# Context attention with its scores transposed: one context position per partition

## The chip, the cores and the metric

The kernel runs on one core of a Trainium2 chip. The metric is the device time of one execution in microseconds (us); the median of several runs is compared. TensorE (PE) multiplies matrices and loads its weights (PEld) beside the products; VectorE (DVE), ScalarE (ACT) and GpSimd (POOL) work elementwise; SyncE (SP) issues the loads.

## The reference, cut to what matters

All data is float32. There are 16 batches of 128 rows with 512 columns, and a context of 2048 positions per batch.

```python
def _L0_xattn_ref(hidden_states, visual_hidden_state):
    scores = jnp.einsum('bld,bvd->blv', hidden_states, visual_hidden_state)
    probs = jax.nn.softmax(scores, axis=-1)
    return jnp.einsum('blv,bvd->bld', probs, visual_hidden_state)
...
x = x + _L0_xattn_ref(_layernorm(x, axis=-1), ctx_1024)
x = x + _L0_attn_ref(_layernorm(x, axis=-1), L0_attn_Wq_down, ...)
x = x + _L0_ffn_ref(_layernorm(x, axis=-1), L0_ffn_Wr, L0_ffn_A, L0_ffn_Bw)
```

The second step is causal self-attention with 16 heads of 32 columns and rotary positions; the third sends each batch through the two of eight low-rank experts that its first row chooses.

## The kernel before

The work of a batch is cut into Python generators, and the kernel's last part calls their steps in an order written out by hand. `score(b)` makes the layer norm of x, its transpose hT, the context scores (psc), their maximum and the exponentials sc. `attend(b)` multiplies the exponentials with the context (av), divides by their sum and adds x. `inner(b)` is the self-attention: q, k and v, the head scores pss, their softmax att, the transposed probabilities (tr_p_a, copied to pT_a), the head outputs y and the output product o. `experts(b)` routes the batch (`shares`, `route`, with the small product lg) and applies the two experts (mid, ffn). `early(b)` routes the last batch ahead of its end.

The 2048 context positions come in four tiles of 512, once turned (ctxT, four at a time in SBUF) for the scores and once as they are (ctx, four at a time) for av. In `score`, a tile takes four products with 512 columns each: the weights are the four column blocks of hT, and the result has one query row per partition and 512 positions along it. VectorE (L220) moves a result from PSUM to sc and takes its maximum along the row in the same instruction. After the fourth tile one ScalarE instruction (L229) makes all 2048 exponentials of a row and their sum.

The product av needs the positions on the partitions. So `attend` transposes the exponentials 128 columns at a time on TensorE (tr_p, through `turn` and `transposed`, L93), and ScalarE copies each group of four out of PSUM (L126). Two groups are turned ahead of the first av.

The order on TensorE and on SP's queue at the start is kept as written. The instructions of the other engines are put in order by a scheduler, which also sets the waits. In the loop of 14 passes, pass b runs `inner(b)`, `attend(b+1)`, `score(b+2)` and `experts(b-1)` in turns. PSUM has eight banks of 512 columns: three in `ps_tr` (transposes and small products), two in `ps_sc` (psc, and the first two of the four head-score banks, pss_sc) and three in `ps_acc` (av, q, k, v, pss_acc, y, o, mid, ffn). A bank is given out again when all readers of its last content are done.

Names of tiles in the profile have no numbers: psc stands for every context score bank, tr_p for every transposed group of exponentials.

Of the kernel before, what the change touches and what calls it, by code (L numbers as in the profile page):

```python
# [11 lines left out]
F32 = mybir.dt.float32  # L12
I32 = mybir.dt.int32
U32 = mybir.dt.uint32
AF = mybir.ActivationFunctionType
ALU = mybir.AluOpType
AX = mybir.AxisListType
PSUM = bass.MemoryType.PSUM

P = 128  # L20
B, S, V, D = 16, 128, 2048, 512
# [3 lines left out]
KC = D // P  # L25
VC = V // 512
# [40 lines left out]
def perceiver_block(ctx: ExitStack, tc: tile.TileContext, io: dict, out: bass.AP):  # L67
    nc = tc.nc

    const = ctx.enter_context(tc.tile_pool(name="const", bufs=1))  # L70
    p1 = ctx.enter_context(tc.tile_pool(name="p1", bufs=1))
    p2 = ctx.enter_context(tc.tile_pool(name="p2", bufs=2))
    p3 = ctx.enter_context(tc.tile_pool(name="p3", bufs=3))
    p4 = ctx.enter_context(tc.tile_pool(name="p4", bufs=4))
    p5 = ctx.enter_context(tc.tile_pool(name="p5", bufs=5))
    ps_tr = ctx.enter_context(tc.tile_pool(name="ps_tr", bufs=3, space=PSUM))
    ps_sc = ctx.enter_context(tc.tile_pool(name="ps_sc", bufs=2, space=PSUM))
    ps_acc = ctx.enter_context(tc.tile_pool(name="ps_acc", bufs=3, space=PSUM))
# [3 lines left out]
    ident = cst[:, C_ID : C_ID + P]  # L82
    ones = const.tile([P, P], F32, name="ones")
# [5 lines left out]
    def matmul(*args, **kwargs):  # L89
        tc.keep_in_program_order(nc.tensor.matmul(*args, **kwargs))  # L90

    def transpose(*args):
        tc.keep_in_program_order(nc.tensor.transpose(*args))  # L93
# [9 lines left out]
    def bank(pool, tag, name):  # L103
        return pool.tile([P, 512], F32, tag=tag, name=name)
# [4 lines left out]
    def layernorm(src, name, n=P, tag="h"):  # L109
        stats = p2.tile([P, 6], F32, tag="stats", name=f"st_{name}")[:n]  # L110
        nc.vector.bn_stats(stats, src)
        mv = p2.tile([P, 2], F32, tag="mv", name=f"mv_{name}")[:n]
        nc.vector.bn_aggr(mv, stats)  # L113
        rstd = p2.tile([P, 1], F32, tag="rstd", name=f"rs_{name}")[:n]
        nc.gpsimd.tensor_scalar_add(rstd, mv[:, 1:2], EPS)  # L115
        nc.gpsimd.tensor_tensor(rstd, rstd, mhalf[:n], ALU.pow)  # L116
        h = (p2 if tag == "h" else p1).tile([P, D], F32, tag=tag, name=f"{tag}_{name}")[:n]
        nc.vector.tensor_scalar(h, src, mv[:, 0:1], rstd, ALU.subtract, ALU.mult)  # L118
        return h

    def transposed(src, dst, name, at=(0, 1, 2, 3)):

        tr = bank(ps_tr, "tr", f"tr_{name}")
        for c, i in enumerate(at):
            transpose(tr[:, c * P : (c + 1) * P], src[:, i * P : (i + 1) * P], ident)
        nc.scalar.copy(dst, tr.rearrange("p (c t) -> p c t", c=4))  # L126

    def turn(src, at, name):
        t = p5.tile([P, 4, P], F32, tag="pT", name=f"pT_{name}")
        transposed(src, t, f"p_{name}", at)  # L130
        return t

# [3 lines left out]
    def load_weight(n, tag="ctxT"):  # L136

        down[n] = []
        for g in range(2):
            t = p4.tile([P, 4, D], F32, tag=tag, name=f"down_{n}_{g}")  # L140
            load(
                t, io[f"W{n}_downT"][g * 512 : (g + 1) * 512].rearrange("(a p) c -> p a c", p=P)
            )
            down[n].append(t)
# [8 lines left out]
    def fold_products(i, n, g):  # L153
        banks = [bank(ps_acc, "acc", f"fold_{n}_{g}_{j}") for j in range(2)]
        for a in range(4):
            for j, ps in enumerate(banks):
                rows = slice(j * L, (j + 1) * L)
                matmul(
                    ps[a * DH : (a + 1) * DH, :], up[rows, i, :], down[n][g][rows, a, :],
                    start=True, stop=True,  # L160
                )
        folded = []
        for j, ps in enumerate(banks):
            t = p5.tile([P, D], F32, tag="pT", name=f"folded_{n}_{g}_{j}")
            (nc.vector.tensor_copy if j else nc.scalar.copy)(t, ps)
            folded.append(t)
        return folded
# [14 lines left out]
    scores, firsts, values, lasts, routes = {}, {}, {}, {}, {}  # L182


    def load_x(b):
        xs[b] = p3.tile([P, D], F32, tag="x", name=f"x_{b}")
        load(xs[b], io["x"][b])
# [3 lines left out]
    def load_turned(b, vs=range(VC)):  # L191
        for v in vs:
            t = p4.tile([P, KC, 512], F32, tag="ctxT", name=f"ctxT_{b}_{v}")
            load(t, io["ctxT"][b, v])
            turned_cts.setdefault(b, []).append(t)
# [11 lines left out]
    def score(b):  # L207

        h = layernorm(xs[b], f"1_{b}")
        yield  # L210
        hT = p2.tile([P, KC, S], F32, tag="hT1", name=f"hT1_{b}")
        transposed(h, hT, f"1_{b}")
        yield
        sc = p2.tile([P, V], F32, tag="sc", name=f"sc_{b}")
        mx = p2.tile([P, VC], F32, tag="mx", name=f"mx_{b}")
        for v, ct in enumerate(turned_cts.pop(b)):
            ps = bank(ps_sc, "sc", f"psc_{b}_{v}")
            for c in range(KC):
                matmul(ps, hT[:, c, :], ct[:, c, :], start=(c == 0), stop=(c == KC - 1))
            nc.vector.tensor_scalar(  # L220
                sc[:, v * 512 : (v + 1) * 512], ps, 1.0, None, ALU.mult, ALU.max,
                accum_out=mx[:, v : v + 1],
            )
            if v < VC - 1:
                yield
        nm = p2.tile([P, 1], F32, tag="nm", name=f"nm_{b}")
        nc.vector.tensor_reduce(nm, mx, AX.X, ALU.max, negate=True)  # L227
        den = p2.tile([P, 1], F32, tag="den", name=f"den_{b}")
        nc.scalar.activation(sc, sc, AF.Exp, bias=nm, accum_out=den)  # L229
        rden = p2.tile([P, 1], F32, tag="rden", name=f"rden_{b}")  # L230
        nc.vector.reciprocal(rden, den)
        scores[b] = (sc, rden)
        yield

    def attend(b):

        sc, rden = scores.pop(b)
        acc = bank(ps_acc, "acc", f"av_{b}")
        turned = [turn(sc, range(4 * i, 4 * i + 4), f"{b}_{i}") for i in range(2)]
        yield  # L240
        for v, ct in enumerate(cts.pop(b)):
            now = turned.pop(0)
            for j in range(4):
                matmul(
                    acc, now[:, j, :], ct[:, j, :],
                    start=(v == 0 and j == 0), stop=(v == VC - 1 and j == 3),
                )
            if v + 2 < VC:
                turned.append(turn(sc, range(4 * (v + 2), 4 * (v + 2) + 4), f"{b}_{v + 2}"))
            if v < VC - 1:  # L250
                yield
        x1 = p2.tile([P, D], F32, tag="x1", name=f"x1_{b}")
        nc.vector.scalar_tensor_tensor(x1, acc, rden, xs.pop(b), ALU.mult, ALU.add)  # L253
        firsts[b] = (x1, layernorm(x1, f"2_{b}"))
        yield

    def inner(b):
# [89 lines left out]
        def heads(c):  # L347
            first = c // 2 * 8 + c % 2 * 2
            return first, first + 1, first + 4, first + 5

        now = [turn(flat, heads(c), f"a_{b}_{c}") for c in range(HC)]
        yield
        acc = bank(ps_acc, "acc", f"y_{b}")
# [139 lines left out]
    def step(kind, b, n=1):  # L493
        if not 0 <= b < B:
            return
        if (kind, b) not in gens:
            gens[kind, b] = kind(b)
        for _ in range(n):
            next(gens[kind, b])
# [10 lines left out]
    step(score, 0, 5)  # L510
    step(score, 1, 2)
    step(score, 0)
    step(score, 1, 3)
    load_weight("q")
    load_weight("k")
    step(attend, 0, 2)
    step(score, 1)
    load_weight("v", "ctx")
    step(attend, 0, 3)
    load_x(2)  # L520
    step(score, 2)
    load_ctx(1, [0, 1])
# [18 lines left out]
    for b in range(B - 2):  # L541
        if 2 < b + 2 < B:
            load_turned(b + 2)
        step(inner, b, 2)
        step(experts, b - 1)
        step(score, b + 2)
        step(inner, b)
        step(experts, b - 1)
        step(score, b + 2, 3)
        step(attend, b + 1)  # L550
        step(inner, b)
        step(attend, b + 1, 2)
        step(score, b + 2)
        step(attend, b + 1)
        step(inner, b)
        step(attend, b + 1)
        if b + 2 < B:
            load_ctx(b + 2)
        if b + 3 < B:
            load_x(b + 3)  # L560
        step(inner, b)
        step(experts, b - 1)
        step(inner, b)
        step(inner, b + 1)
        step(experts, b - 1)
        step(score, b + 3)


    y, z = B - 2, B - 1
    step(inner, y, 2)  # L570
    step(experts, y - 1)
    step(inner, y)
    step(experts, y - 1)
    step(attend, z, 5)
    step(inner, y)
    step(experts, y - 1)
    step(inner, z)
    step(experts, y - 1)
    step(inner, z, 3)
    step(inner, y)  # L580
    step(early, z)
    step(inner, y)
    step(inner, z)
# [53 lines left out]
```

## Time and profile before

| | us |
|---|---|
| median of 3 runs | 886.39 |
| lowest and highest | 885.8, 887.42 |
| the profiled execution | 886.97 |
| its span, first to last instruction | 885.0 |
| mean granted TensorE clock | 0.994 of full speed |

Costly groups by line, of the profiled execution:

| line, engine | what | count | busy us | mean ns |
|---|---|---|---|---|
| L90 PE | av<-ctx,pT, 128x512 | 512 | 231.6 | 596 |
| L90 PE | psc<-ctxT,hT, 128x512 | 512 | 228.6 | 600 |
| L90 PE | q<-hT,w_q, 128x128 | 512 | 62.6 | 282 |
| L93 PE | tr_p<-cst,sc, 128x128 | 256 | 35.8 | 273 |
| L220 DVE | sc<-psc, 128x512 | 64 | 44.3 | 692 |
| L126 ACT | pT<-tr_p, 128x512 | 64 | 34.2 | 580 |
| L229 ACT | sc<-sc, 128x2048 | 16 | 32.1 | 2004 |

A product counts as two records on TensorE and on its weight loads, a transpose as one. Products are pipelined: a record is longer than the distance to the next one, so the cost of a stretch of TensorE is read from the starts. Times of engines other than TensorE overlap with it.

### The profile page before, as it was taken

Reading aid. Unit: us, or ns where it says so; the run is one execution under the profiler, and the core shown is the slowest. Engines: PE = TensorE matmul, PEld = TensorE weight load, DVE = VectorE, ACT = ScalarE, POOL = GpSimd, SP = SyncE. Lnnn points to the kernel's source line nnn. Section 1 sums busy time; section 2 is a strip of 40 time slices with the busy share of each in tenths; the row PEclk is TensorE's granted clock in tenths of the full one; section 3 lists DMA queues with packets and bytes.
Section 4 is the critical chain, followed back from the end, with each engine's and each line's share of the span. In section 5 each row is a group of like instructions: output and inputs, shape, how many; then the busy total and the mean of one; then the engine's idle time right before and its main releaser. Section 6 shows DMA issues by size and latency. Waiting matters only on the chain.

```text
span 885.0 us, 11267 instructions
## 1 busy us (share of the span) xinstructions
PE 857.5 (97%) x4138; PEld 503.1 (57%) x4138; DVE 429.1 (48%) x1122; ACT 265.1 (30%) x797; POOL 168.7 (19%) x232
## 2 busy tenths in 40 slices
PE   5999999999999999999999999999999999999896
PEld 2446564565657556565755656575565657556653
DVE  1135455354645535464453546446354644633563
ACT  0132413315142331514233151422315142241351
POOL 1001021130403103040210404021040402204124
PEclk9999999999999999999999999999999999999998
DMA  6997735646273564627356362745636273151002
GB/s 274 414 367 302 258 122 207 215 145 225 79 278 137 199 217 143 230 80 269 146 191 226 137 235 78 265 155 183 233 134 235 78 263 148 34 181 37 12 1 72
DMA packets 29542, 159.39 MB, mean 180 GB/s; under 512 B 4144, under 2 KB 4400, under 8 KB 13104
## 3 DMA queue, kind: packets, MB, share of 16 engines
q1 hardware_dynamic: 25392, 146.09, 44.6%
q0 software_dynamic: 4096, 12.59, 4.5%
q8 instruction: 33, 0.54, 0.2%
q14 instruction: 21, 0.17, 0.1%
HBM read 154.47 MB, written 4.19 MB: 179 GB/s over the span
## 4 chain that ended last, share of the span: by engine, by line
PE 94%; DVE 2%; ACT 1%; DMA 1%; POOL 1%; issue 1%; POOLq 0%; SPq 0%; ACTq 0%
PE psc L90 25%; PE av L90 25%; PE q L90 7%; PE k L90 6%; PE v L90 6%; PE o L90 5%; PE tr_p_a L93 3%; PE tr_p L93 3%; PE tr L93 2%; PE pss_sc L90 2%; PE y L90 2%; PE mid L90 2%; PE pss_acc L90 1%; PE ffn L90 1%; ACT att L335 1%; DMA x<-in_x_dram 1%
## 5 line engine op out<-in xcount | busy, mean ns | idle before, releaser
L90 PE MATMUL av<-ctx,pT 128*128 128x512 f32 x512 | 231.6, 596 | 0.5 <-ACT pT L126 0.5
L90 PE MATMUL psc<-ctxT,hT 128*128 128x512 f32 x512 | 228.6, 600 | 0.7 <-ACT hT L126 0.7
L90 PEld LDWEIGHTS psc<-ctxT,hT 128*128 128x128 f32 x512 | 95.9, 192 | 110.8 <-issue 109.8
L90 PEld LDWEIGHTS av<-ctx,pT 128*128 128x128 f32 x512 | 93.5, 190 | 105.6 <-issue 104.6
L220 DVE TENSOR_SCALAR_CACHE_REDUCE sc<-psc 128x512 f32<-128x512 f32 x64 | 44.3, 692 | 162.0 <-PE psc L90 162.0
L335 ACT ACTIVATE att<-att,nmx 128x128 f32<-128x128 f32 x256 | 99.0, 388 | 46.1 <-DVE nmx L333 46.1
L115 POOL TENSOR_SCALAR rs<-mv 128x1 f32<-128x1 f32 x48 | 10.7, 234 | 487.9 <-DVE mv L113 487.4
L126 ACT COPY hT<-tr 128x512 f32<-128x512 f32 x48 | 26.8, 587 | 196.2 <-PE tr L93 196.2
L126 ACT COPY pT<-tr_p 128x512 f32<-128x512 f32 x64 | 34.2, 580 | 157.2 <-PE tr_p L93 157.1
L90 PEld LDWEIGHTS q<-hT,w_q 128*128 128x128 f32 x512 | 60.0, 196 | 13.5 <-ACT hT L126 13.5
L90 PE MATMUL q<-hT,w_q 128*128 128x128 f32 x512 | 62.6, 282 | 4.0 <-ACT hT L126 4.0
L90 PE MATMUL o<-w_c,yT 128*128 128x512 f32 x128 | 59.5, 609 | 1.1 <-ACT yT L362 1.1
L90 PE MATMUL k<-hT,w_k 128*128 128x128 f32 x512 | 59.8, 275 | 0.0
L253 DVE SCALAR_TENSOR_TENSOR x<-av,rden,x 128x512 f32<-128x512 f32 x16 | 12.0, 751 | 97.9 <-PE av L90 97.9
L90 PEld LDWEIGHTS k<-hT,w_k 128*128 128x128 f32 x512 | 58.5, 192 | 0.0
L90 PE MATMUL v<-w_v,hT 128*128 128x512 f32 x128 | 57.6, 592 | 0.0
L118 DVE TENSOR_SCALAR h<-x,mv,rs 128x512 f32<-128x512 f32 x48 | 39.3, 819 | 37.3 <-POOL rs L116 36.3
L229 ACT ACTIVATE sc<-sc,nm 128x2048 f32<-128x2048 f32 x16 | 32.1, 2004 | 53.2 <-DVE nm L227 53.2
L335 ACT ACTIVATION_READ_ACCUMULATOR att<-att,nmx 128x1 f32 x256 | 47.9, 187 | 0.0
L93 PEld LDWEIGHTS tr_p<-cst,sc 128*128 128x128 f32 x256 | 31.0, 141 | 24.7 <-issue 24.7
L340 DVE TENSOR_TENSOR att<-att,rsm 128x512 f32<-128x512 f32 x64 | 44.1, 689 | 1.0
L407 POOL DMA_INDIRECT each<-in_A_dram,g_blocks x32 | 32.7, 1023 | 58.9 <-DVE g_dn L424 50.4
(114 smaller groups left out, 913.3 us busy)
## 6 DMA issues: line engine op xcount, KB each, us to landing
ctxT<-in_ctxT_dram SPq DMA_DIRECT2D x64, 1024.0 KB, 5.2
ctx<-in_ctx_dram SPq DMA_DIRECT2D x64, 1024.0 KB, 4.8
x<-in_x_dram SPq DMA_DIRECT2D x16, 256.0 KB, 5.8
out_dram<-out POOLq DMA_DIRECT2D x15, 256.0 KB, 2.4
down_q<-in_Wq_downT_dram SPq DMA_DIRECT2D x2, 1024.0 KB, 10.6
down_k<-in_Wk_downT_dram SPq DMA_DIRECT2D x2, 1024.0 KB, 8.3
down_v<-in_Wv_downT_dram SPq DMA_DIRECT2D x2, 1024.0 KB, 7.9
w_c<-in_Wc_dram SPq DMA_DIRECT2D x1, 1024.0 KB, 14.0
```

The costliest lines, as they stand in the source:

```text
L90: tc.keep_in_program_order(nc.tensor.matmul(*args, **kwargs))
L93: tc.keep_in_program_order(nc.tensor.transpose(*args))
L115: nc.gpsimd.tensor_scalar_add(rstd, mv[:, 1:2], EPS)
L118: nc.vector.tensor_scalar(h, src, mv[:, 0:1], rstd, ALU.subtract, ALU.mult)
L126: nc.scalar.copy(dst, tr.rearrange("p (c t) -> p c t", c=4))
L220: nc.vector.tensor_scalar(sc[:, v * 512 : (v + 1) * 512], ps, 1.0, None, ALU.mult, ALU.max, accum_out=mx[:, v : v + 1],)
L229: nc.scalar.activation(sc, sc, AF.Exp, bias=nm, accum_out=den)
L253: nc.vector.scalar_tensor_tensor(x1, acc, rden, xs.pop(b), ALU.mult, ALU.add)
L335: nc.scalar.activation(att[:, i, :], att[:, i, :], AF.Exp, bias=nmx[:, i : i + 1], scale=SCALE, accum_out=sm[:, i : i + 1],)
L340: nc.vector.tensor_tensor(att[:, hs, :], att[:, hs, :], rsm[:, hs, None].to_broadcast([P, 4, S]), ALU.mult)
L407: nc.gpsimd.indirect_dma_start(each[:, i, :], None, io["A"], bass.IndirectOffsetOnAxis(ap=blocks[:, i : i + 1], axis=0),)
```

## The change

The context scores are computed with the roles of the two operands exchanged. The weights are now 128x128 blocks of ctxT, the moving side is a block of hT with 128 columns, and a result has one context position per partition and the 128 query rows along it. A tile takes 16 products in place of 4. These scores lie as av needs them, so `attend` has no transposes and no copies of transposes.

The maximum and the sum of a query row now run across partitions. ScalarE copies each score bank to sc (L224), and VectorE takes the elementwise maximum over the tiles from PSUM (L227), then halves 512 to 128 columns in two steps (L232, L233). A transpose on TensorE (tr_m), a reduction along the row (L242), a diagonal matrix of the negative maxima (L244) and a product with ones (spread) bring each query's maximum to all partitions. VectorE adds it to the four parts of sc (L249), and ScalarE makes the exponentials of each part (L252). VectorE adds up the parts (L255 to L258); in `attend`, a product of this partial sum with ones (den) gives the sum of each row, whose reciprocal (L276) is used as before.

`score` has two steps more and `attend` one less, and the written order is changed to fit. In the loop the context scores of a batch are now split two and two around the head scores and the first av, where they were three and one; `attend` starts after the head scores. At the end, `attend` of the last batch takes turns with the head scores of the batch before. The tag pT has four buffers in place of five. What is loaded stays the same.

```diff
-            ps = bank(ps_sc, "sc", f"psc_{b}_{v}")
-            for c in range(KC):
-                matmul(ps, hT[:, c, :], ct[:, c, :], start=(c == 0), stop=(c == KC - 1))
-            nc.vector.tensor_scalar(
-                sc[:, v * 512 : (v + 1) * 512], ps, 1.0, None, ALU.mult, ALU.max,
-                accum_out=mx[:, v : v + 1],
-            )
+            ps = bank(ps_sc, "sc", f"psc_{b}_{v}").rearrange("p (j t) -> p j t", j=4)
+            for j in range(4):
+                for c in range(KC):
+                    matmul(
+                        ps[:, j, :], ct[:, c, j * P : (j + 1) * P], hT[:, c, :],
+                        start=(c == 0), stop=(c == KC - 1),
+                    )
+            nc.scalar.copy(sc[:, v], ps)
+
+            if v:
+                nc.vector.tensor_tensor(mx, ps, mx if v > 1 else sc[:, 0], ALU.max)
             if v < VC - 1:
                 yield
+
+        def halved(t, op):
+            nc.vector.tensor_tensor(t[:, :2], t[:, :2], t[:, 2:], op)
+            nc.vector.tensor_tensor(t[:, 0], t[:, 0], t[:, 1], op)
+            return t[:, 0]
+
+        most = halved(mx, ALU.max)
+        yield
+
+        tr = bank(ps_tr, "tr", f"tr_m_{b}")
+        transpose(tr[:, :S], most, ident)
         nm = p2.tile([P, 1], F32, tag="nm", name=f"nm_{b}")
-        nc.vector.tensor_reduce(nm, mx, AX.X, ALU.max, negate=True)
-        den = p2.tile([P, 1], F32, tag="den", name=f"den_{b}")
-        nc.scalar.activation(sc, sc, AF.Exp, bias=nm, accum_out=den)
-        rden = p2.tile([P, 1], F32, tag="rden", name=f"rden_{b}")
-        nc.vector.reciprocal(rden, den)
-        scores[b] = (sc, rden)
+        nc.vector.tensor_reduce(nm, tr[:, :S], AX.X, ALU.max, negate=True)
+        diag = p1.tile([P, S], F32, tag="diag", name=f"diag_{b}")
+        nc.vector.tensor_scalar(diag, ident, nm, None, ALU.mult)
+        yield
+        spread = bank(ps_tr, "tr", f"spread_{b}")
+        matmul(spread[:, :S], ones, diag, start=True, stop=True)
+        for v in range(VC):
+            nc.vector.tensor_tensor(
+                sc[:, v], sc[:, v], spread[:, None, :S].to_broadcast([P, 4, S]), ALU.add
+            )
+            nc.scalar.activation(sc[:, v], sc[:, v], AF.Exp)
+        sums = p1.tile([P, 4, S], F32, tag="sums", name=f"sums_{b}")
+        for v in range(1, VC):
+            nc.vector.tensor_tensor(sums, sc[:, v], sums if v > 1 else sc[:, 0], ALU.add)
+        part = p2.tile([P, S], F32, tag="part", name=f"part_{b}")
+        nc.vector.tensor_tensor(sums[:, :2], sums[:, :2], sums[:, 2:], ALU.add)
+        nc.vector.tensor_tensor(part, sums[:, 0], sums[:, 1], ALU.add)
+        scores[b] = (sc, part)
         yield
...
-        turned = [turn(sc, range(4 * i, 4 * i + 4), f"{b}_{i}") for i in range(2)]
-        yield
         for v, ct in enumerate(cts.pop(b)):
-            now = turned.pop(0)
             for j in range(4):
                 matmul(
-                    acc, now[:, j, :], ct[:, j, :],
+                    acc, sc[:, v, j, :], ct[:, j, :],
                     start=(v == 0 and j == 0), stop=(v == VC - 1 and j == 3),
                 )
-            if v + 2 < VC:
-                turned.append(turn(sc, range(4 * (v + 2), 4 * (v + 2) + 4), f"{b}_{v + 2}"))
+            if v == VC - 2:
+                den = bank(ps_tr, "tr", f"den_{b}")
+                matmul(den[:, :1], part, ones[:, :1], start=True, stop=True)
+                rden = p2.tile([P, 1], F32, tag="rden", name=f"rden_{b}")
+                nc.vector.reciprocal(rden, den[:, :1])
...
         step(score, b + 2)
         step(inner, b)
         step(experts, b - 1)
-        step(score, b + 2, 3)
+        step(score, b + 1)
+        step(score, b + 2, 2)
+        step(inner, b)
         step(attend, b + 1)
-        step(inner, b)
-        step(attend, b + 1, 2)
+        step(score, b + 2)
+        step(attend, b + 1)
         step(score, b + 2)
         step(attend, b + 1)
         step(inner, b)
+        step(score, b + 2)
         step(attend, b + 1)
...
     y, z = B - 2, B - 1
-    step(inner, y, 2)
+    step(inner, y)
+    step(score, z)
+    step(inner, y)
     step(experts, y - 1)
     step(inner, y)
     step(experts, y - 1)
-    step(attend, z, 5)
+    step(attend, z)
     step(inner, y)
+    step(attend, z, 3)
     step(experts, y - 1)
+    step(inner, y)
     step(inner, z)
     step(experts, y - 1)
     step(inner, z, 3)
-    step(inner, y)
```

In the start, which the diff leaves out here, the steps of `score` for batches 0 and 1 take turns in the same manner.

More of the change, by code (lines that the diff above doesn't have):

```diff
@@ L74, in perceiver_block @@
     p4 = ctx.enter_context(tc.tile_pool(name="p4", bufs=4))
-    p5 = ctx.enter_context(tc.tile_pool(name="p5", bufs=5))
     ps_tr = ctx.enter_context(tc.tile_pool(name="ps_tr", bufs=3, space=PSUM))
@@ L128, in turn @@
     def turn(src, at, name):
-        t = p5.tile([P, 4, P], F32, tag="pT", name=f"pT_{name}")
+        t = p4.tile([P, 4, P], F32, tag="pT", name=f"pT_{name}")
         transposed(src, t, f"p_{name}", at)
@@ L163, in fold_products @@
         for j, ps in enumerate(banks):
-            t = p5.tile([P, D], F32, tag="pT", name=f"folded_{n}_{g}_{j}")
+            t = p4.tile([P, D], F32, tag="pT", name=f"folded_{n}_{g}_{j}")
             (nc.vector.tensor_copy if j else nc.scalar.copy)(t, ps)
@@ L213, in score @@
         yield
-        sc = p2.tile([P, V], F32, tag="sc", name=f"sc_{b}")
-        mx = p2.tile([P, VC], F32, tag="mx", name=f"mx_{b}")
+        sc = p2.tile([P, VC, 4, S], F32, tag="sc", name=f"sc_{b}")
+        mx = p1.tile([P, 4, S], F32, tag="mx", name=f"mx_{b}")
         for v, ct in enumerate(turned_cts.pop(b)):
-            ps = bank(ps_sc, "sc", f"psc_{b}_{v}")
-            for c in range(KC):
-                matmul(ps, hT[:, c, :], ct[:, c, :], start=(c == 0), stop=(c == KC - 1))
-            nc.vector.tensor_scalar(
-                sc[:, v * 512 : (v + 1) * 512], ps, 1.0, None, ALU.mult, ALU.max,
-                accum_out=mx[:, v : v + 1],
-            )
+            ps = bank(ps_sc, "sc", f"psc_{b}_{v}").rearrange("p (j t) -> p j t", j=4)
[8 more added lines that the diff above has]
+                nc.vector.tensor_tensor(mx, ps, mx if v > 1 else sc[:, 0], ALU.max)
@@ L233, in score @@
+        nc.vector.tensor_tensor(part, sums[:, 0], sums[:, 1], ALU.add)
+        scores[b] = (sc, part)
         yield
     def attend(b):
-        sc, rden = scores.pop(b)
+        sc, part = scores.pop(b)
         acc = bank(ps_acc, "acc", f"av_{b}")
-        turned = [turn(sc, range(4 * i, 4 * i + 4), f"{b}_{i}") for i in range(2)]
-        yield
         for v, ct in enumerate(cts.pop(b)):
-            now = turned.pop(0)
             for j in range(4):
                 matmul(
-                    acc, now[:, j, :], ct[:, j, :],
+                    acc, sc[:, v, j, :], ct[:, j, :],
@@ L512, in perceiver_block @@
     step(score, 0)
-    step(score, 1, 3)
+    step(score, 1)
+    step(score, 0)
+    step(score, 1)
+    step(score, 0)
+    step(score, 1)
     load_weight("q")
     load_weight("k")
-    step(attend, 0, 2)
+    step(attend, 0)
+    step(score, 1)
+    step(attend, 0)
     step(score, 1)
     load_weight("v", "ctx")
-    step(attend, 0, 3)
+    step(attend, 0, 2)
     load_x(2)
```

## The prediction

> **What bounds the kernel now.** I read the busy times first, then the waits, then the timeline of TensorE over one batch of the steady loop, since a share over the whole span does not say which stage pays.
>
> ```profile
> PE 857.5 (97%) x4138; PEld 503.1 (57%) x4138; DVE 429.1 (48%) x1122; ACT 265.1 (30%) x797; POOL 168.7 (19%) x232
> ```
>
> TensorE is the bound; VectorE and ScalarE have half their time to spare. In the waits, TensorE itself waits 26 us in all, none of it repeated once per batch, and the only per-batch wait of its weight loads that touches the changed code is this one:
>
> ```profile
> PEld pss_sc L90 <- DVE sc L220: 2.4, 14, 0.2
> ```
>
> It says that in 14 batches the head scores pss, which share the two PSUM banks of ps_sc with the context scores psc, had to wait 0.2 us for the eviction of a psc. The timeline of TensorE (start, length, operation, count) from the routing product lg to the head outputs y of one batch:
>
> ```profile
> 237.56 0.28 PE L90 MATMUL lg<-g_part,ones 128*128 128x8 f32 x2
> 237.70 10.55 PE L90 MATMUL psc<-ctxT,hT 128*128 128x512 f32 x24
> 248.08 1.04 PE L93 MATMUL tr_p<-cst,sc 128*128 128x128 f32 x8
> 249.05 1.13 PE L90 MATMUL pss_sc<-kb,qT 64*128 64x256 f32 x8
> 250.01 1.03 PE L90 MATMUL pss_acc<-kb,qT 64*128 64x256 f32 x8
> 250.97 3.70 PE L90 MATMUL av<-ctx,pT 128*128 128x512 f32 x8
> 254.51 0.60 PE L93 MATMUL tr_p<-cst,sc 128*128 128x128 f32 x4
> 258.38 0.60 PE L93 MATMUL tr_p<-cst,sc 128*128 128x128 f32 x4
> 258.82 3.60 PE L90 MATMUL psc<-ctxT,hT 128*128 128x512 f32 x8
> 262.26 3.60 PE L90 MATMUL av<-ctx,pT 128*128 128x512 f32 x8
> 271.04 1.08 PE L90 MATMUL y<-pT_a,vv 128*32 128x128 f32 x32
> 277.78 3.82 PE L90 MATMUL q<-hT,w_q 128*128 128x128 f32 x32
> 281.43 3.74 PE L90 MATMUL k<-hT,w_k 128*128 128x128 f32 x32
> 285.01 1.04 PE L93 MATMUL tr<-cst,h 128*128 128x128 f32 x8
> ```
>
> No idle time stands in it, so a price on TensorE is the step from one start to the next. One 512-wide context tile costs 262.26 - 258.82 = 3.44 us (8 records are 4 products). The transposes tr_p cost 0.97 + 0.44 + 0.44 = 1.85 us. And q and k are exactly the form that the new scores take, 16 products with a 128x128 weight and 128 columns: 3.65 and 3.58 us. lg to y is 33.48 us. The period of the loop is 289.32 - 237.56 = 51.76 us.
>
> **Products (loop).** Per batch: 16 transposes go, -1.85. Four tiles go from 3.44 to 3.57 (k's rate), +0.52; at q's rate +0.84. Added: the transpose of the maxima (0.11, a sixteenth of tr_p_a's 1.82), the spread product (a sixteenth of k, 0.22), the sum product den (like lg, 0.14): +0.47. Products alone: -0.86 us per batch.
>
> **The wait that is added.** Before, after the last psc of the group came 0.97 us of tr_p, which covered the eviction: a psc ends issuing at 248.08, VectorE starts at 248.28, is done at 248.97, and pss_sc runs at 249.05.
>
> ```profile
> 248.28 0.69 DVE L220 TENSOR_SCALAR_CACHE_REDUCE sc<-psc 128x512 f32<-128x512 f32 x1 [2.73 <-PE psc L90]
> 237.76 0.59 ACT L292 COPY vv<-v 128x512 f32<-128x512 f32 x1 [2.80 <-PE v L90]
> ```
>
> After, TensorE's order is lg, spread, psc 0, psc 1, pss, av 0, psc 2, av 1, psc 3, av 2, den, tr_p_a, maxima, av 3. The transposes no longer stand between psc and pss; the first pss (0.24 us) takes the bank of psc 0, free since long, the second that of psc 1, which ended 0.24 us before. Psc 1 now has two readers, the copy on ScalarE (L224) and the maximum on VectorE (L227); in the built program the maximum waits for the copy of the same bank, and the second pss for the maximum. So, from psc 1's last issue: 0.20 to ScalarE's start (237.56 to 237.76 above), 0.59 copy, 0.03 (ScalarE's last exponential ends at 257.64, VectorE goes on at 257.67), 0.69 maximum (the 128x512 add out of PSUM, L326, has 685 ns), 0.08 back to TensorE: 1.59. Minus the 0.24 of the first pss, plus about 0.05 for a weight load that is not hidden: 1.40 us of idle TensorE per batch. Queued behind it are pss, all four av and the rest of the batch.
>
> The Trainium skill, PSUM — Partial Sum Buffer, section "PSUM bank collisions raise a hardware error", says that two engines must not read one bank at once. No trace here has two readers of a bank; by that rule the wait is unavoidable for this code, and without it, with the two reads side by side, the sum would have 0.78 in place of 1.40.
>
> **Is VectorE there in time?** From the spread on it holds four adds (0.60 apart, as the two L326 adds that take 1.29), about 2.4 of routing operations between them, three sums (two of them dependent, 0.73), a 256-wide half (0.42), a 128-wide one. I bound that last by a kb quarter (0.42) and a four-column operation (0.16), and take 0.25. Starting at 238.19 these end near 244.7; psc 1 ends at 245.1 and its copy at 245.9: VectorE has 1.2 us of slack, ScalarE more (four exponentials of 512 columns, bounded by 0.39 for 128 and 2.00 for 2048 of them, on the line between these 0.71 each). Were nothing overlapped, the maximum would be 0.3 late: upper bound of the wait 1.7; lower bound 0.78 if ScalarE's copy did not count (0.20 + 0.69 + 0.08 - 0.24 + 0.05). Kb is made before the spread, so pss has it.
>
> **Covered otherwise.** The chain psc 3, copy, maximum, two halves takes 2.3 us and has av 2, den and tr_p_a (5.4) in front of the transpose that needs it. Its reduction and the diagonal (bounds 0.16 and 0.82) have until the next batch's spread. The division needs den before x1: av 3 lies between. Loads: the same tiles on SP's queue; the third and fourth ctxT tile are released later by some us, with 50 us to the next use. Cost nothing.
>
> So per batch: -0.86 + 1.40 = +0.54. The bounds give -0.08 (wait 0.78) and +1.16 (wait 1.7 and q's rate). Fourteen loop batches: +7.6 us, from -1 to +16.
>
> **Start.** Eight tiles +1.0, tr_p -1.85 and its 0.24 us wait for the copy, small products +0.6: -0.4, with every maximum hidden behind the next tile.
>
> **End.** Before, pss of batch 14 stands after av of batch 15, and q of batch 15 waits for its layer norm and behind ScalarE's exponentials:
>
> ```profile
> 826.76 0.63 PE L93 MATMUL tr<-cst,h 128*128 128x128 f32 x4 [0.89 <-DVE h L118]
> 831.62 5.46 PE L90 MATMUL q<-hT,w_q 128*128 128x128 f32 x32 [3.37 <-ACT hT L126]
> 859.56 3.22 PE L93 MATMUL tr_p_a<-cst,att 128*128 128x128 f32 x16
> ```
>
> The first two waits are 0.89 and 3.37, and q then takes 5.46 in place of 3.65; the granted clock there is 0.62. After, pss 14 comes behind the first av, so that the exponentials are done when av ends, and tr_p_a of batch 14 (1.82) moves into the layer norm's time. Counted from the end of q 14 (799.03): before, pss of batch 15 runs at 847.84, 48.8 later. After: the spread of batch 15 puts adds and sums into VectorE's queue ahead of g_share and g_part, so that lg comes near 10.4 in place of 7.7 (2.7 of new idle); then av 0 to 14.1, pss 16.0, av and den 26.5, mid and tr_p_a 29.4, tr near 30.1, q 31.4 to 35.0, k 38.6, v 42.1, tr_v after vv's copy (0.85 idle) 43.9, y 44.9. Gain 3.9, or 2.1 if the 2.7 us of idle costs the clock as the 3.37 did. I take 3.0. Behind it the chain is the same.
>
> **Sum.** +7.6 - 0.4 - 3.0 = +4.2 us on the profiled execution (span 885.0, its own time 886.97): 891.2. The median of the runs, 886.39, lies 0.58 below it: 890.6.
>
> **Rivals.** *Clock:* TensorE drops its clock in each new wait. For it: before the tr_p_a at 859.56 stands a wait of 2.08 us, and its 16 transposes took 3.22 where 1.98 is usual (clock 0.63). Against it: after waits of 0.70 and 0.68 us (117.67, 122.48) products kept their rate, and 1.4 lies nearer to those and stands among full work. It decides if one wait of 1.4 is enough; then 14 x 1.24 more, 908. The Trainium skill, TensorE: Matmul & The Clock Gate, Part 1, has the clock fall after an idle window of about 3.4 us; by that rule this rival is out and 890.6 stands.
>
> *Faster:* the wait is one eviction of 0.78, not two in a row. For it: before, VectorE alone kept the bank only 0.9 us. Against: the built program's wait. Then -0.08 x 14 - 0.4 - 3.0 = -4.5: 881.9. If the wait vanished, -0.86 x 14 - 3.4 = -15.4: 871.
>
> *No change:* wait at 1.2 and the end at its best (-3.9): 14 x 0.34 - 4.3 = +0.5: 886.9.
>
> **Chances.** My forecast with its spread 0.65, clock 0.08, faster 0.15, no change 0.12. A measurement of this kernel tells 0.2% (1.8 us) from no change: slower 0.71, within 0.13, faster 0.16. Range: below, it reaches into the faster case, to 882; above, the forecast with q's rate for the tiles (+4.5) and a late maximum (+4), less what the end can give: 898. Left out are the clock, and a wait that vanishes.
>
> **What would show it.** Right: psc near 3.57 us a tile, 16 tr_p gone, a wait of pss_sc for L227 of about 1.3 to 1.4 us in each of 14 batches, a period of 52.3, clock 1.0 there, an idle of near 2.7 before lg of batch 13. Wrong: a period below 51.8, the wait below 0.9, psc above 3.7 a tile, or a clock below 1 after the wait.

## The result, and the profile after

The changed kernel takes 902.71 us (median; 900.42 to 903.56), beside 886.74 us for the kernel before, run beside it: a ratio of 1.0177, 95% interval 1.0155 to 1.0198. It is slower, as forecast, but by 16 us in place of 4, and outside the range (882 to 898). The profiled execution has 903.06 us and a span of 901.1, against 885.0 before. These 16.1 us fall as follows; the ends of the stretches are starts of products in the two traces.

| stretch | before, us | after, us | difference | forecast |
|---|---|---|---|---|
| up to q of batch 0 | 71.65 | 71.60 | -0.05 | -0.4 |
| q of batch 0 to q of batch 14 (14 loop batches) | 723.73 | 741.61 | +17.88 | +7.6 |
| q of batch 14 to pss of batch 15 | 52.46 | 48.68 | -3.78 | -3.0 |
| from there to the end | 37.17 | 39.20 | +2.03 | 0 |

So the loop holds the miss. The busy line of the profile page comes first again, then the waits of the weight loads and of TensorE itself that touch the changed code (us in total, times, longest us):

```profile
PE 858.8 (95%) x5498; PEld 623.9 (69%) x5498; DVE 510.8 (57%) x1234; ACT 272.1 (30%) x829; POOL 171.6 (19%) x232
```

```profile
PEld pss_sc L89 <- DVE mx L227: 22.5, 14, 1.7
PE pss_sc L89 <- DVE mx L227: 16.9, 14, 1.3
...
PE lg L89 <- DVE g_part L412: 3.1, 2, 2.3
```

TensorE is busy for no longer than before (858.8 against 857.5) and idle for 15 us more. The wait of pss_sc for the maximum is there in each of the 14 batches, where it was forecast. The same batch as before, on TensorE:

```profile
241.31 0.47 PE L89 MATMUL spread<-diag,ones 128*128 128x128 f32 x2
241.61 7.31 PE L89 MATMUL psc<-hT,ctxT 128*128 128x128 f32 x64
248.85 0.70 PE L89 MATMUL pss_sc<-kb,qT 64*128 64x256 f32 x2
250.78 0.91 PE L89 MATMUL pss_sc<-kb,qT 64*128 64x256 f32 x5 [1.23 <-DVE mx L227]
...
252.70 3.70 PE L89 MATMUL av<-ctx,sc 128*128 128x512 f32 x8
256.24 3.73 PE L89 MATMUL psc<-hT,ctxT 128*128 128x128 f32 x32
259.81 3.60 PE L89 MATMUL av<-ctx,sc 128*128 128x512 f32 x8
```

A transposed score tile steps 259.81 - 256.24 = 3.57 us, exactly k's rate. The 16 transposes are gone. The eight head-score products run from 248.85 to 252.70, 3.85 us where they took 250.97 - 249.05 = 1.92: 1.93 us of TensorE is lost, of which the line puts 1.23 down to the maximum; the rest stands in longer records beside the gap (the two ahead of it are drawn 0.70 long, where two of them step 0.24). The forecast had 1.40 for the whole.

The two evictions of the bank (ScalarE, then VectorE):

```profile
249.42 0.58 ACT L224 COPY sc<-psc 128x512 f32<-128x512 f32 x1 [3.39 <-PE psc L89]
```

```profile
250.03 0.69 DVE L227 TENSOR_TENSOR mx<-psc,sc 128x512 f32<-128x512 f32 x1 [1.68 <-ACT sc L224]
```

They are 0.58 and 0.69 long and 0.03 apart, as forecast. But the copy starts 0.57 us after the first pss (248.85), though the product it waits for was issued before that. In the first batch of the loop the same copy starts 0.10 after its pss (90.18 and 90.08), and there the wait on TensorE is 0.78, not 1.23:

```profile
91.55 0.91 PE L89 MATMUL pss_sc<-kb,qT 64*128 64x256 f32 x5 [0.78 <-DVE mx L227]
```

The semaphore events of the trace (a semaphore is the signal by which an engine tells another that its work is done) say the same: from the start of the last psc product to its signal it is 0.29 us in the first batch and 0.73 to 0.77 in the 13 others. SyncE's load of a ctxT tile, which waits for the same products, starts together with the copy in both places (249.41 and 90.18), so it is the signal that is late, not ScalarE. The granted clock is 1.00 over the whole loop, so no clock is lost in it.

### The profile page after: what moved, and what is told of

Its sections match the earlier page's. It is cut to its first block, busy times and chain, and to the rows that moved or that the text cites. A ratio compares the mean times of both kernels' runs of the same rounds, so it can differ in the third digit from the quotient of the medians.

```text
span 901.1 us, 14130 instructions
## 1 busy us (share of the span) xinstructions
PE 858.8 (95%) x5498; PEld 623.9 (69%) x5498; DVE 510.8 (57%) x1234; ACT 272.1 (30%) x829; POOL 171.6 (19%) x232
## 3 DMA queue, kind: packets, MB, share of 16 engines
q1 hardware_dynamic: 25392, 146.09, 44.9%
## 4 chain that ended last, share of the span: by engine, by line
PE 92%; DVE 3%; ACT 2%; POOL 1%; issue 1%; DMA 1%; SPq 0%; ACTq 0%; POOLq 0%
PE psc L89 26%; PE av L89 25%; PE q L89 6%; PE o L89 6%; PE k L89 6%; PE v L89 6%; PE tr_p_a L92 3%; PE tr L92 2%; PE pss_sc L89 2%; PE y L89 2%; PE mid L89 2%; PE ffn L89 1%; PE pss_acc L89 1%; DVE mx L227 1%; ACT sc L224 1%
## 5 line engine op out<-in xcount | busy, mean ns | idle before, releaser
L89 PEld LDWEIGHTS psc<-hT,ctxT 128*128 128x128 f32 x2048 | 237.5, 194 | 14.9 <-issue 13.9
L89 PE MATMUL psc<-hT,ctxT 128*128 128x128 f32 x2048 | 239.1, 277 | 0.7 <-ACT hT L125 0.7
L89 PE MATMUL av<-ctx,sc 128*128 128x512 f32 x512 | 231.8, 596 | 0.0
L89 PEld LDWEIGHTS av<-ctx,sc 128*128 128x128 f32 x512 | 93.1, 192 | 97.6 <-issue 97.6
L224 ACT COPY sc<-psc 128x512 f32<-128x512 f32 x64 | 37.1, 580 | 161.8 <-PE psc L89 160.3
L227 DVE TENSOR_TENSOR mx<-psc,mx 128x512 f32<-128x512 f32 x32 | 22.0, 688 | 88.9 <-ACT sc L224 88.9
L117 DVE TENSOR_SCALAR h<-x,mv,rs 128x512 f32<-128x512 f32 x48 | 39.6, 825 | 37.2 <-POOL rs L115 36.3
L434 POOL DMA_INDIRECT each<-in_A_dram,g_blocks x32 | 35.4, 1106 | 89.1 <-DVE g_dn L451 84.0
L125 ACT COPY pT_a<-tr_p_a 128x512 f32<-128x512 f32 x64 | 33.0, 599 | 49.2 <-PE tr_p_a L92 49.1
L249 DVE TENSOR_TENSOR sc<-sc,spread 128x512 f32<-128x512 f32 x64 | 42.7, 680 | 5.2 <-PE spread L89 5.2
L252 ACT ACTIVATE sc<-sc 128x512 f32<-128x512 f32 x64 | 40.2, 631 | 16.6 <-DVE sc L249 15.7
```

Of the source, the lines that this page charges most:

```text
L224: nc.scalar.copy(sc[:, v], ps)
L227: nc.vector.tensor_tensor(mx, ps, mx if v > 1 else sc[:, 0], ALU.max)
L249: nc.vector.tensor_tensor(sc[:, v], sc[:, v], spread[:, None, :S].to_broadcast([P, 4, S]), ALU.add)
L252: nc.scalar.activation(sc[:, v], sc[:, v], AF.Exp)
L434: nc.gpsimd.indirect_dma_start(each[:, i, :], None, io["A"], bass.IndirectOffsetOnAxis(ap=blocks[:, i : i + 1], axis=0),)
```

## The experiments

The theory after the result: the loop loses by the wait for the bank of the second psc, which is two evictions in a row plus a late signal. Rivals: the products cost more than counted; another wait stands behind this one. The first four kernels take these apart. Each starts from the changed kernel unless it says otherwise.

**1. Cover the wait (e1_av_first).** In the loop:

```diff
         step(score, b + 2, 2)
-        step(inner, b)
         step(attend, b + 1)
+        step(inner, b)
```

> In the loop the first av of batch b+1 is issued before the head scores pss of batch b, so that 3.5 us of products stand between the second psc and the pss that takes its bank. Theory (the loss in the loop is the wait of pss for the bank, 1.93 us of idle TensorE per batch, the late start of the copy in it): the wait goes whole, the period falls from 53.04 to about 51.1 us, 14 x 1.93 = 27 us less than the changed kernel, near 876 us, faster than the kernel before by about 11. Rival 1 (the products themselves cost more than counted, by weight loads at the new tile's start): the period stays above 52 and the time above 888. Rival 2 (the wait moves: av waits for its exponentials or its bank instead): about 1 us of wait per batch shows before av, and the time is near 890.

Measured: 875.43 us, ratio to the kernel before 0.988 (0.9847 to 0.9912). The period falls from 53.04 to 51.13. TensorE in the same batch:

```profile
235.11 7.31 PE L89 MATMUL psc<-hT,ctxT 128*128 128x128 f32 x64
242.26 3.60 PE L89 MATMUL av<-ctx,sc 128*128 128x512 f32 x8
245.79 1.13 PE L89 MATMUL pss_sc<-kb,qT 64*128 64x256 f32 x8
...
247.72 3.84 PE L89 MATMUL psc<-hT,ctxT 128*128 128x128 f32 x32
```

The idle time is gone and nothing takes its place: the head scores step 247.72 - 245.79 = 1.93 us, as before the change. Both rivals fall as sources of the 1.93 us. The signal is still late in 13 batches here (0.75 us), which now costs nothing. The period without the wait, 51.13 against 51.76, also gives the price of the products by themselves: -0.63 us per batch.

**2. One reader of the bank (e2_max_from_copy).**

```diff
-                nc.vector.tensor_tensor(mx, ps, mx if v > 1 else sc[:, 0], ALU.max)
+                nc.vector.tensor_tensor(mx, sc[:, v], mx if v > 1 else sc[:, 0], ALU.max)
```

> The maximum reads the copy in SBUF instead of the PSUM bank, so that the bank has one reader, ScalarE's copy, and the order of instructions is as in the changed kernel. Theory (two reads in a row hold the bank, 0.58 and 0.69 us): the wait per batch shrinks by the maximum, 0.69 plus its hand-over of 0.03, to about 1.2 us of idle; 14 x 0.72 = 10 us less than the changed kernel, near 892.5. The head-score wait is then named after the copy, L224. Rival (the wait is set by something that ends last whatever the readers, the late start of the copy's release): less than 3 us gained.

Measured: 890.75 us, ratio 1.0044 (1.0031 to 1.0057); period 52.33, 0.71 less than the changed kernel. The wait names the other engine now, and is 0.5 us long where it was 1.25:

```profile
PE pss_sc L89 <- ACT sc L224: 6.7, 13, 0.5
```

So the second reader costs its own length, as the forecast's chain had it.

**3 and 4. The late signal (e3_gather_later, e4_no_gather).** In the 13 batches with the late signal, GpSimd issues the indirect loads of the experts' weights at this point; in the first batch it has none to issue. Experiment 3 has two additions ahead of them in the program:

```diff
+        for _ in range(2):
+            nc.gpsimd.tensor_tensor(
+                each.rearrange("p i r -> p (i r)"), cst[:, 0:512],
+                row.to_broadcast([P, TOP * KC * R]), ALU.add,
+            )
```

Experiment 4 replaces all three indirect loads, the first two like this:

```diff
-            nc.gpsimd.indirect_dma_start(
-                each[:, i, :], None, io["A"],
-                bass.IndirectOffsetOnAxis(ap=blocks[:, i : i + 1], axis=0),
-            )
+            nc.gpsimd.dma_start(each[:, i, :], io["A"][i * P : (i + 1) * P])
```

> Two additions on GpSimd of 512 columns (about 1.27 us each, of no use to the result) are put ahead of the routing's indirect loads, so that these begin some 2.5 us later in each batch; all else is as in the changed kernel. In 13 loop batches of the changed kernel ScalarE's copy of the second psc starts 0.46 us later than in the first batch, and GpSimd's indirect loads end about 0.5 us ahead of it. Theory A (the end of psc reaches ScalarE late because the indirect loads are under way): the last psc product to its signal falls from 0.75 to 0.29 us in these batches, and the time by 13 x 0.46 = 6 us, to near 896.5. Theory B (the delay belongs to TensorE's own queue at this point, whatever GpSimd does): 0.75 stays, the time is within 1 us of the changed kernel, or above it where the experts' weights come late.

> The experts' weights are loaded by plain loads from fixed places on GpSimd's queue in place of the three indirect ones; this leaves out the choice of the experts, the products are the same. Theory A (indirect loads under way delay the signal of the second psc): 0.75 becomes 0.29 us, 13 x 0.46 = 6 us less than the changed kernel, near 896.5. Theory B (the delay is TensorE's own): 0.75 stays, within 1 us of the changed kernel. A third way (any load issued by GpSimd does it): 0.75 stays here but goes where the loads are issued later.

Without indirect loads (e4): 895.5 us, ratio 1.0093 (1.0072 to 1.0114), ScalarE's copy starts 0.31 us after the start of the last psc product in all 14 batches (0.75 to 0.79 in the 13 late ones of the changed kernel), the wait is 0.78 in each, the period 52.59. Theory B falls, and the size is as forecast: 0.45 us in 13 batches. But the plain loads need no routing result, and GpSimd issues them some 30 us later (279 to 283 in the batch whose first pss stands at 248.68). So this kernel has no load at all beside the signal: it shows that the loads cause the delay, not that it takes indirect ones, and the third way is not tested.

In e3 the signal is on time in all 14 batches (0.29), yet the time is 924.59 us (ratio 1.0442, 1.042 to 1.0464), 28 us above what A expected. The loads did not simply move as meant: the scheduler put that of the second expert matrix (wb) between the two additions, so that it ends 0.89 us ahead of the first pss, and the other two behind them. So e3 too has the delay gone with the loads moved, but it does not show that moving them later is what ends it. The last load stands here:

```profile
250.62 0.95 POOL L439 DMA_INDIRECT each<-in_A_dram,g_blocks  x1 [0.30 <-issue]
```

It ends at 251.57, and 0.04 us later the signal of a head-score product arrives, 0.40 us after that product's start, which is its usual time. Experiments 8 and 9 below come back to this.

The experiment disturbed two other things. First, GpSimd's additions slow VectorE's sums, and the maximum queues behind these:

```profile
246.68 2.75 DVE L255 TENSOR_TENSOR sums<-sc,sums 128x512 f32<-128x512 f32 x2
...
250.14 0.68 DVE L227 TENSOR_TENSOR mx<-psc,sc 128x512 f32<-128x512 f32 x1
```

The two sums take 2.75 us where they take 1.49 in the changed kernel; GpSimd's second addition runs beside them, from 247.82 to 248.88. The Trainium skill, SBUF — State Buffer, section "Who interferes with whom", says that a VectorE instruction with two inputs in SBUF contends with a GpSimd instruction that reads SBUF; this row agrees.

Second, the wait of 1.48 us is long enough to cost the clock in some batches. TensorE in one of them, and then the windows from its first pss on (window, length, busy time of each engine; the last three values are the granted clock, the DMA share and GB/s):

```profile
357.46 0.91 PE L89 MATMUL pss_sc<-kb,qT 64*128 64x256 f32 x5 [1.48 <-DVE mx L227]
...
360.29 4.44 PE L89 MATMUL av<-ctx,sc 128*128 128x512 f32 x8
```

```profile
355.30:359.60 4.30, 2.83 (x16) 2.15 (x16) 3.43 (x7) 0.58 (x1) 2.26 (x3) 0.86 0.86 282
359.60:363.00 3.40, 3.40 (x7) 1.41 (x7) 3.18 (x9) 1.85 (x10) 0.00 (x0) 0.68 0.51 188
```

The clock is 0.86 in the window of the wait and 0.68 in the next, and av takes 4.44 us for 3.70. Five periods of this run are 54.93 long in place of 53.29. An equally long wait in another batch (1.49 at 250.88) cost nothing, and neither did any in the changed kernel, the longest of which is 1.25. The end is 5 us longer too, where mid waits up to 2.0 us for the experts' weights. The profiled execution, 918.83 us, is the fastest of this kernel; in four of the five others the mean clock is 0.968 to 0.971, for 0.976 in it, so they probably lost more to the clock, which no trace shows.

**5. The wait at the end (e5_av_first_end).** Experiment 1 and:

```diff
     y, z = B - 2, B - 1
-    step(inner, y)
     step(score, z)
+    step(inner, y)
```

> As the first experiment (first av ahead of the head scores), and at the end the spread of the last batch is issued ahead of q of batch 14 instead of behind it, so that VectorE's additions and sums of the last batch are done before the routing sums that lg of batch 13 waits for. Theory (that wait of 2.33 us comes from these additions and sums in VectorE's queue, and the slow av after it, 5.38 in place of 3.68, from the idle): 2.3 to 4 us less than the first experiment's 875.4, so 871.5 to 873. Rival (lg waits for the layer norm's chain anyway, as q and k of batch 14 leave too little time): less than 1 us gained.

Measured: 873.72 us, ratio 0.9839 (0.982 to 0.9858); the intervals of this and of experiment 1 meet, so the times alone don't separate them. The profiled spans are 870.3 and 873.8, and the stretch from q of batch 14 to pss of batch 15 goes from 50.39 to 46.73:

```profile
798.53 0.36 PE L89 MATMUL lg<-g_part,ones 128*128 128x8 f32 x2 [0.69 <-DVE g_part L412]
798.74 3.68 PE L89 MATMUL av<-ctx,sc 128*128 128x512 f32 x8
```

The wait falls from 2.33 to 0.69, as the theory says, and the av behind it from 5.38 to 3.68. The second part is not shown to be due to the shorter wait: behind a wait of 2.32 to 2.34 us that av took 5.38 in experiments 1, 4, 6 and 8, but 3.68 in the changed kernel and in experiments 2, 3, 7, 9 and 10. Of the 3.66 us of the stretch, 0.22 are the spread, which now stands ahead of it. This is the fastest version found.

**6 and 7. What in the indirect loads delays the signal (e6_gather_shift, e7_two_gathers).**

```diff
+        late = small(b, TOP, "late", I32)
+        nc.gpsimd.tensor_copy(late, blocks)
+        blocks = late
```

That is experiment 6, ahead of the indirect loads; experiment 7 has

```diff
-        nc.gpsimd.indirect_dma_start(
-            wb, None, io["BT"], bass.IndirectOffsetOnAxis(ap=rows, axis=0)
-        )
+        nc.gpsimd.dma_start(wb, io["BT"][:P])
```

> One copy of two columns on GpSimd is put ahead of the three indirect loads, which shifts them by some 0.2 us, order and all else as in the changed kernel. Theory A1 (the signal of the second psc is held until about 0.53 us after the last indirect instruction's end): product to signal grows by the shift, from 0.75 to about 0.95 us, and the time by 13 x 0.2 = 2.6 us, to about 905. Theory A2 (a fixed cost of 0.46 us whenever indirect loads are under way): 0.75 stays and the time is within 1 us of the changed kernel.

> The last of the three indirect loads, that of the second expert matrix, is replaced by a plain load from a fixed place; this leaves out the choice of the rows of that matrix, the products are the same. The two indirect loads left end 1.3 us earlier, near 1 us before the last psc product. Theory A1 (the signal waits for the last indirect instruction's end plus 0.53): product to signal is 0.29 us in all batches, near 895.5 as without any indirect load. Theory A2 (any indirect load near by costs 0.46): 0.75 stays, near 902.

Both give the same: 895.59 us, ratio 1.0087 (1.0064 to 1.011), and 895.6, ratio 1.0088 (1.0066 to 1.011); signal after 0.29 us in every batch, wait 0.78, period 52.59. So neither form of theory A1 or A2 stands whole: e7 speaks for A1, but e6 against both. In e7 the plain load is issued at another place too (281.81), so beside the signal it is simply absent. GpSimd and ScalarE in e6, where the first pss stands at 246.75:

```profile
243.20 1.64 POOL L437 DMA_INDIRECT each<-in_A_dram,g_late  x1 [0.28 <-DVE g_rows L431]
245.14 1.17 POOL L437 DMA_INDIRECT each<-in_A_dram,g_late  x1 [0.30 <-issue]
246.61 0.96 POOL L442 DMA_INDIRECT wb<-in_BT_dram,g_rows  x1 [0.30 <-issue]
```

```profile
246.86 0.59 ACT L224 COPY sc<-psc 128x512 f32<-128x512 f32 x1 [2.93 <-PE psc L89]
```

The copy starts on time in the middle of the third indirect instruction. In the changed kernel, that instruction ends 0.03 after the first pss, just before the signal is due, and the copy starts 0.54 us after it:

```profile
247.92 0.96 POOL L439 DMA_INDIRECT wb<-in_BT_dram,g_rows  x1 [0.31 <-issue]
```

The shift also turned out larger than the copy: the last load ends 0.8 us later, since the first indirect instruction became longer (1.64 for 1.09).

**8 and 9. A finer shift (e8_two_copies, e9_three_copies).** Two and three chained copies in place of one in e6.

> Two chained copies of two columns on GpSimd ahead of the indirect loads in place of one, so that these come about 0.2 us later than in the sixth experiment. There the second of three indirect instructions ends 0.53 us before the signal of the second psc is due. Theory B1 (a signal that falls due within some 0.5 us after the end of any indirect instruction is held until then): with the end 0.33 us before, product to signal is about 0.48 us, the period about 52.8. Theory B2 (only the end of the last of them does it): 0.29, the period 52.59.

> Three chained copies in place of one, about 0.4 us later than in the sixth experiment; the second indirect instruction then ends about 0.1 us before the signal is due. Theory B1: product to signal about 0.68 us, the period near 53.0. Theory B2: 0.29, the period 52.59.

One run each: 896.87 and 895.92 us, signal after 0.29 us, period 52.59 in both. By themselves they don't decide between B1 and B2, because the instructions did not land where they were meant to. With two copies the first indirect instruction is shorter (1.37) and the second ends 0.53 us before the signal is due, as in e6. With three, VectorE's sums stretch the third copy to 0.67, the first indirect instruction ends 1.2 us before that point and the second 0.06 after it.

Other signals of the same traces speak against both theories as they were put. In e3 the head scores' signal falls due 0.04 to 0.07 us behind the end of the last indirect load and comes on time in 11 of 13 batches (0.02 us late at most); in the two others it is 0.25 late, behind products that ran at a granted clock of 0.69 and 0.63. At the end of the changed kernel two of these signals come on time 0.02 and 0.07 us behind the end of the wb load (832.86 and 832.91, end 832.84). So an end shortly before the signal is not enough for a delay.

**10. Both terms at once (e10_copy_and_shift).** The edits of experiments 2 and 6.

> Two edits together: the maximum reads the copy in SBUF (as in the second experiment), and one copy of two columns on GpSimd is put ahead of the indirect loads (as in the sixth). If the second reader of the bank and the late signal are two separate terms of the wait, the period falls by both from 53.04: by 0.72 and 0.46 to about 51.87, and the time to about 890.75 - 6 = 884.5 to 885.5, some 1.5 to 2 us below the kernel before. If they are not separate (one covers the other), the time stays near 890.

Measured: 885.48 us, ratio 0.9984 (0.9973 to 0.9996); period 51.86, for 51.87 expected. The two terms add up.

## Why the prediction was wrong

**Products: sign right, 0.23 too good.** Forecast -0.86 us per batch; experiment 1 shows -0.63. The tiles were exact (3.57). Mis-sized were the small steps: the spread takes 241.61 - 241.31 = 0.30 for 0.22, the transpose of the maxima 0.17 for 0.11 (272.19 to 272.36), and the rest is lost in steps under 0.1. A sixteenth of a run of 16 products is too low a price for one product that stands alone.

**The wait: the chain was right, its first link was not.** The step that failed is "0.20 to ScalarE's start", taken from an eviction at another place of the batch, after v and lg. At its own place the link takes 0.57 us (248.85 to 249.42) in 13 of 14 batches, where it is 0.10 with the signal on time (first batch, e4): 0.46 us for a late signal that the sum did not have. It costs 13 x 0.46 = 6.0 us, and from q of batch 0 to q of batch 14 the kernels e4, e6 and e7, which remove it, take 735.6 us for 741.61; their medians are 7 us below the changed kernel.

Without the late signal the wait is 3.39 - 1.92 = 1.47 us (e4), beside 1.40 forecast, and that copy, hand-over and maximum stand in it is shown by experiment 2. That these two numbers lie so close is in part luck. The first link was 0.10 shorter than forecast, but the 0.24 of the first pss did not come off: from the second pss to av it is 252.07 - 250.15 = 1.92 us in e4, as long as all the head scores take without a wait.

The upper bound of 1.7 came from a late VectorE, another cause. VectorE was in fact early: its last sum ended at 248.35, 1.65 us before the copy did. The time from the first add to that end was 6.54 us (241.81 to 248.35), which fits the 6.5 between 238.19 and 244.7 of the prediction; the terms listed there add up to 7.5, so the list is about 1 us too long for its own result. The waits of TensorE before the change add up to 22.8 us where the prediction says 26; no term of its sum uses this.

**The loop's sum.** -0.63 + 1.47 + 0.46 = +1.30 for a batch with the late signal, where the period gives 1.28: of the 10.3 us by which the loop missed, 6 are the late signal and about 4 the small terms (0.23 + 0.07 per batch). The start gave -0.05 in place of -0.4; which of its terms was off is not shown.

**The end: right.** The gain was -3.8, within the 2.1 to 3.9 that were worked out, and lg of batch 13 had its new idle time of 2.32 (forecast 2.7), 1.6 of it put there by VectorE's additions and sums, as experiment 5 shows. Counted from the end of q 14 (816.88), pss of batch 15 comes 45.0 us later, for 44.9 in the forecast. Both ends of the range occurred: in the changed kernel the av behind the idle took 3.68 at a granted clock of 1.00; in experiment 1 the same av took 5.38 at 0.68 and the stretch gave only -2.1. Which of the two a run gets was not foreseen; the 3.0 lay between them.

**"Behind it the chain is the same": true of the instructions, not of the time.** From pss of batch 15 to the end the changed kernel has the same work and takes 2.03 more. Its first o there:

```profile
882.56 6.42 PE L89 MATMUL o<-w_c,yT 128*128 128x512 f32 x8 [0.32 <-ACT yT L389]
```

Before, this product took 5.31. The granted clock over this stretch is 0.75, for 0.89 before; a wait of 2.08 us stands in it in both. In the experiments, e3 aside, the same stretch with the same code took 36.3 to 39.2 us, and the 37.2 from before the change lies inside that. So the 2.03 go with a slower clock in this one execution, and nothing shows them as a cost of the change. The prediction had no term for it.

**Rivals.** The rival *clock* did not come true: the granted clock is 1.00 in the loop. But e3 shows how near it was: with waits of 1.48 us the clock fell in 5 batches. The Trainium skill, TensorE: Matmul & The Clock Gate, Part 1, gives an idle window of about 3.4 us, and the prediction put the rival out by it; e3 has the fall after a wait well short of that (1.48 us as drawn, 2.17 from one pss start to the next), so here the measurement decides. *Faster* and *no change* needed a wait of 0.78 and 1.2; it was 1.93. Their direction was reachable by another order: the transposed scores are worth 11 us when the wait is covered.

**The range** lacked any term for a signal that arrives later than the row it was read from. The bounds were drawn around what each engine does, not around the hand-over between two of them; with 13 x 0.46 us for it the upper end would have been 904.

## What to carry to other kernels

When a step that stands between a product and the next user of its bank is removed, ask first what else could stand there: moving one block of 3.5 us of independent products turned a loss of 16 us into a gain of 11. A chain of hand-overs should be priced at the place where it will stand, with what the other queues are doing then, and with a margin for each link. A second reader of a PSUM bank that is waited for cost its full length here (0.71 us per batch), so it is better served from the copy.

## What was not expected of the hardware

Beside GpSimd's indirect loads, a signal from TensorE reached ScalarE 0.46 us late in 13 of 13 batches, and was on time when the loads were absent, one fewer, or shifted by 0.8 us. What holds it is open. It came on time in the middle of such an instruction (e6), and late when it fell due within 0.1 us after the end of the last one, that of wb. But signals of the head scores that fell due as close behind such an end came on time (11 batches of e3, and two signals at the end of the changed kernel). What else it takes (these products, their reader, or the order of the loads) is not shown.

In these traces the length of a wait alone does not decide whether the clock falls: 1.48 us cost it in one batch of e3 and 1.49 did not in another, and 2.3 us before lg cost it in experiment 1 and not in the changed kernel.
